# Means stored as whole rows from the edge loops of a graph network, and partitions that load successive rows

## The chip, the cores and the metric

The kernel runs on one core of one Trainium2 chip. The core has five engines that each take their instructions in order and wait for one another by semaphores: TensorE (PE, matrix products and the turning of blocks, with PEld for its weight loads), VectorE (DVE), ScalarE (ACT), GpSimd (POOL, which here issues the gathers from DRAM) and SyncE (SP, which here issues all other DMAs). The metric is the device time of one execution in microseconds. Before the change three runs took 10164.5, 10168.21 and 10176.87 us, the median is 10168.21 us. All values are float32 unless said otherwise.

## What is computed

There are 10,000 nodes with 64 features, and 160,000 directed edges with 64 features each, sorted by target node. A network of four GENConv layers is followed by one attention layer; both have residual connections. What matters here is what happens on the edges:

```python
def _genconv(x, src, dst, ea, W1, b1, lg, lb, W2, b2, t):
    m = relu(x[src] + ea) + EPS
    logits = m * t
    mx = segment_max(logits, dst)
    e = exp(logits - mx[dst])
    denom = segment_sum(e, dst)
    agg = segment_sum(m * (e / denom[dst]), dst)    # a mean of m with weights e
    h = agg + x
    ...

def _L1_gnn_ref(x, edge_attr, edge_index, WQ, bQ, WK, bK, WE, bE, WV, bV):
    ...
    score = Kh[src] * Qh[dst] * inv_sqrt_d * Eh
    score = exp(clip(score.sum(-1, keepdims=True), -5.0, 5.0))
    return segment_sum(Vh[src] * score, dst)
```

Each GENConv layer is an edge part (`softmax_layer`) and a node part (`node_layer`); the attention layer has an edge part (`attention_layer`) and leaves its sums to a last node part.

## The kernel before

**Tiling.** The edges lie in two halves. The first half is read forward on partitions 0 to 63 (one partition for each of the 64 features), the second half is read backward on partitions 64 to 127. So a tile of 128 partitions by 512 columns holds 512 edges of each half. A chunk is such a tile (CE = 512 columns in CG = 4 groups of G = 128). There are NC = 158 chunks: 155 of 512 columns, then two of 256 and one of 128.

**One chunk in `softmax_layer`.** `fetch` issues on SP the loads of `marks` (two DMAs, L797, saying where a new target begins) and of `ea`, the edge features (L766). In layer 0 the features come as rows of edges instead (`load_rows`, L773 and L775); PE turns them into columns (`turn_rows`, L784 and L785), ACT copies them out of PSUM (L788) and SP stores them in `eaT` (L789) for the later layers. `front` issues eight gathers of 128 rows on POOL (`xg`, L756), then PE forms z from the features (L829) and adds the turned gathered rows (L831). ACT makes the logits lg in two operations (L834, L835). A scan on DVE follows the running maximum u (L841), a subtraction (L843) leaves the difference to it, and ACT derives `up` (L846) and e (L848, L849). `decay` makes `dec` on ACT (L856). `back` runs one chunk later on DVE: the weighted message `me` (L869), the scan `se` of the weights (L871) and the scan `sm` of the weighted messages (L874). The last column of a target's run of edges holds its denominator in `se` and its numerator in `sm`. Then two 32 by 32 block transposes (L900) turn both, so that 64 channels of sums and weights of one edge can be stored as a row of `st0` (L904): four DMAs of 32 partitions, each with 512 runs of 256 bytes in a full chunk.

**Buffers.** z has five PSUM banks in layers 1 to 3 (three called z, and `ept` and `hist`), three in layer 0, where the others are in use. `lg`, `dec` and `oe` have one bank each. In SBUF `xg` has 7 buffers, `marks` 6, `ea` 4, `so` 3, `u`, `up`, `e`, `se` and `sm` 2, `me` 1.

**Order.** `InOrder` (L68) holds every engine to the order in which the code emits its instructions. In the loop (L906 to L938) one turn emits: `fetch(k+3)`, `front(k)`, the columns of chunk k+2, in layer 0 the counting of edges for the row indices (one-hot tiles on DVE, products on PE), `back(k-1)`, `decay(k)`.

**`node_layer`.** Gathers, for each group of up to 8 x 128 nodes, the row of `st0` at the node's last edge in each half: sums and weights, 128 numbers (`fetch`, L955). `divide` (L962) takes Ln and Exp of the weights on ACT (L967, L968) and multiplies on DVE (L969). Then follow the layer norms and products. `rows_of_nodes` (L496) works out the row indices (`ends`) once, in layer 0. A node without edges in a half reads the one extra row at the end of `st0`, which holds constants.

**`attention_layer`.** Per chunk: `fetch` loads marks, queries (`q`, L1141, a row for each edge in `qs`) and features; `ahead` turns the queries on PE (L1151), forms the edge part (L1154), scans the queries along the edges (L1156) and multiplies (L1160). `scores` turns the gathered keys and values (`kv`, 8 gathers in two `xg` buffers), multiplies (L1183) and sums over heads on PE (L1185); `weights` clips (L1191) and takes the exponential on ACT (L1192); `back` runs a chunk later: product (L1199), scan (L1201), one transpose (L1212), and four stores (L1216) of 512 runs of 128 bytes into `st1`.

Of the kernel before, what the change touches and what calls it, by code (L numbers as in the profile page):

```python
# [9 lines left out]
F32 = mybir.dt.float32  # L10
# [16 lines left out]
def kernel(ctx: ExitStack, tc: tile.TileContext, a, out):  # L27
# [142 lines left out]
    empty = const.tile([1, D2 + D], F32, name="empty")  # L170
    for h in range(2):
        nc.gpsimd.memset(empty[:, h * D:h * D + 32], 1.0)
        nc.gpsimd.memset(empty[:, h * D + 32:(h + 1) * D], -EPS)
    nc.gpsimd.memset(empty[:, D2:], 0.0)
    zeros = const.tile([P, 500], F32, name="zeros")
    nc.gpsimd.memset(zeros, 0.0)
    later.append((st0[2 * HALF:2 * HALF + 1, :], empty[:, 0:D2]))
    later.append((st1[2 * HALF:2 * HALF + 1, :], empty[:, D2:]))

    def load(name, shape, ap):  # L180
        t = const.tile(shape, F32, name=name)
# [314 lines left out]
    def rows_of_nodes(pool, ph):  # L496

        def t(name):
            return pool.tile([P, NT], F32, name="rn_" + name, bufs=1)
        V = nc.vector  # L500
        cnt = t("cnt")
        V.tensor_copy(cnt, ph)
        upto, before = place_nodes(pool, cnt, "ept")
        some = t("some")
        V.tensor_scalar(some, cnt, 0.0, None, op0=OP.is_gt)
        ra, rb, inb = t("ra"), t("rb"), t("inb")
        V.tensor_scalar(inb, before, float(HALF), None, op0=OP.is_ge)
# [8 lines left out]
        V.tensor_scalar_add(ends, ra, float(2 * HALF))  # L516

        ba, bb, spare = t("ba"), t("bb"), t("spare")
# [250 lines left out]
    def load_rows(k, ea_rows):  # L769
        g0, n, cols = span(k)  # L770
        er = edge.tile([P, 2, CG, D], F32, name="er", bufs=3)
        e1 = NE - g0 * G
        nc.sync.dma_start(er[:, 0, :n, :],  # L773
                          ea_rows[g0 * G:(g0 + n) * G, :].rearrange("(g p) d -> p g d", p=G))
        nc.sync.dma_start(er[:, 1, :n, :],  # L775
                          ea_rows[e1 - n * G:e1, :].rearrange("(g p) d -> p g d", p=G))
        return er

    def turn_rows(k, er):

        g0, n, cols = span(k)
        pt = ps("ept", [P, CE])
        for g in range(n):
            nc.tensor.matmul(pt[:D, g * G:(g + 1) * G], er[:, 0, g, :], ident, start=True, stop=True)  # L784
            nc.tensor.matmul(pt[D:, g * G:(g + 1) * G], er[:, 1, n - 1 - g, :], anti,  # L785
                             start=True, stop=True)
# [11 lines left out]
        return t  # L798

    V, S = nc.vector, nc.scalar  # L800

    def softmax_layer(l, ea_rows=None):

# [61 lines left out]
        def back(k, z, u, dec, e):  # L865
# [11 lines left out]
            if k == NC - 1:  # L877
# [15 lines left out]
                for i, t in ((1, se), (2, sm)):  # L893
                    V.tensor_mul(far[:, i:i + 1], far[:, i:i + 1], top[:, 3:4])
                    V.scalar_tensor_tensor(t[:D, m - 1:m], fin[:D, i:i + 1], top[:, 2:3],
                                           far[:, i:i + 1], op0=OP.mult, op1=OP.add)

            so = edge.tile([P, CE // 32, 2, 32], F32, name="so", bufs=3)
            for i, t in ((0, se), (1, sm)):
                V.transpose(so[:, :m // 32, i, :], t[:, :m].rearrange("p (b e) -> p b e", e=32))  # L900
# [14 lines left out]
        for k in range(NC):  # L915
# [18 lines left out]
            if l == 1 and k % 4 == 0:  # L934
                clear_queries(k // 4)
            order()
        back(NC - 1, *held)
        order()  # L938

    def node_layer(l):  # L940
# [21 lines left out]
        @stage  # L962
        def divide(my, g, i0, n, c):
            q = 2 * pairs(n)
            t = my["g"][:, :q].rearrange("p n (h i c) -> p n h i c", h=2, i=2)
            my["h"] = h = work.tile([P, GRP, D], F32, name="n_h", bufs=2)
            S.activation(t[:, :, :, 0, :], t[:, :, :, 0, :], AF.Ln)  # L967
            S.activation(t[:, :, :, 0, :], t[:, :, :, 0, :], AF.Exp, scale=-1.0)  # L968
            V.tensor_mul(h[:, :q, :].rearrange("p n (h c) -> p n h c", h=2), t[:, :, :, 1, :], t[:, :, :, 0, :])  # L969

        @stage
        def enter(my, g, i0, n, c):
# [128 lines left out]

        for g in range(3):
            fetch(g)
        divide(0)
        for i in range(NG2 + (4 if last else 3)):
            span_narrow(i - 3)
            widen(i - 1)
# [5 lines left out]
            spans(i - 1)  # L1113
            relu_narrow(i - 3)
            square(i - 2)
            divide(i + 1)
            back(i - 3)
            root_wide(i - 1)
            leave(i - 3)
# [14 lines left out]
    def attention_layer():  # L1134
# [3 lines left out]
        def fetch(k):  # L1138
            g0, n, cols = span(k)
            q = edge.tile([P, CG, 2, D], F32, name="q", tag="er", bufs=3)  # L1140
            nc.sync.dma_start(  # L1141
                q[:, :n], qs[2 * g0 * G:2 * (g0 + n) * G, :].rearrange("(g p s) d -> p g s d", p=G, s=2))
            return load_marks(k, keeps_d), q, load_ea(k)

        def ahead(k, keep, q, ea):
# [2 lines left out]
            m = n * G  # L1148
            pq = ps("oe", [P, CE])
            for g in range(n):  # L1150
                nc.tensor.matmul(pq[:, g * G:(g + 1) * G], q[:, g, :, :].rearrange("p s d -> p (s d)"),  # L1151
                                 ident, start=True, stop=True)
# [42 lines left out]
        def back(k, keep, pv, sc):  # L1195
# [8 lines left out]
            if k == NC - 1:  # L1204
# [17 lines left out]
        for k in range(NC):  # L1222
            kvs = fetch_kv(k)
            if k + 2 < NC:
                got.append(fetch(k + 2))
            pv, psc = scores(k, kvs, made)
            if held is not None:
                back(k - 1, *held)
            held = got[k][0], pv, weights(k, psc)
            if k + 1 < NC:  # L1230
                made = ahead(k + 1, *got[k + 1])
            order()
        back(NC - 1, *held)
        order()

    puts = []
# [69 lines left out]
```

## Time and profile before

| what | us |
|---|---|
| median of three runs | 10168.21 |
| the profiled execution: its time | 10256.79 |
| its span on the core | 10254.7 |
| layer 0, first to last scan of u (L841) | 1823.57 |
| layer 1, the same | 1810.51 |
| layer 2, the same | 1804.37 |
| layer 3, the same | 1804.35 |
| attention, first to last scan of its sums (L1201) | 1783.61 |
| mean granted TensorE clock over the span, as a share of full speed | 0.629 |

The five stretches of the table hold 9026 us of the span. Between them lie the node parts, some 190 us each, in which 79 gathers read `st0`. A page of the profile lists busy time by engine, groups of instructions by line and tile, and waits by what ended them; the timeline lists single instructions in the order of their start, with in brackets the idle time of that engine just before. "remote" as the end of a wait means a semaphore of another engine that the records don't tie to one instruction; "issue" means that the profile shows nothing that was waited for.

Single durations that the text uses: ACT operations on 128 by 512 take 0.56 to 0.75 us, on 128 by 256 0.34 to 0.42 us; L843 0.70 us, the transposes of L900 0.67 to 0.69 us, the scans L841, L871 and L874 1.26 to 1.28 us; L967, L968 and L969 0.62, 0.63 and 0.69 us; a gather on POOL 0.94 us.

### The profile page before, as it was taken

The numbers are of one execution on the slowest core, as the hardware profiler recorded it, in microseconds if no ns is written. First come the engines' busy times: TensorE is split into PE (matmuls) and PEld (weight loads), VectorE is DVE, ScalarE is ACT, GpSimd is POOL, SyncE is SP. The second block draws the span as 40 slices with busy tenths as digits, with TensorE's granted clock in tenths as the row PEclk, the third lists the DMA queues.
The fourth block names the chain that finished last, engine by engine and source line by source line (L and its number), as shares of the span: only waits on it lengthen the run. The fifth ranks groups of instructions, "written<-read, shape, count | busy, mean of one in ns | idle before, by whom it ended". The sixth has DMA issues, their size and how long they took to land. (4 is left out here: it accounts for less than half of the span.)

```text
span 10254.7 us, 67417 instructions
## 1 busy us (share of the span) xinstructions
PE 4014.2 (39%) x15762; PEld 2685.3 (26%) x15762; DVE 5449.4 (53%) x7473; ACT 2805.0 (27%) x4803; POOL 6358.1 (62%) x6760
## 2 busy tenths in 40 slices
PE   3554445443333333433333343333333444444452
PEld 2333333222222221222222221222222233333331
DVE  3777677535555554355555543555555445545453
ACT  2333333333333333333333342333333310000000
POOL 4566666556666665566666646666666456666665
PEclk6666666665555556665666575555555667777776
DMA  3555555524555554244444433444444235555553
GB/s 89 113 125 123 123 124 123 123 59 119 125 125 129 128 124 109 62 102 105 104 104 103 105 78 71 105 105 104 103 104 106 62 92 122 125 123 126 122 128 82
DMA packets 2462634, 1103.63 MB, mean 108 GB/s; under 512 B 2039472, under 2 KB 2254438, under 8 KB 2462239
## 3 DMA queue, kind: packets, MB, share of 16 engines
q1 hardware_dynamic: 2247039, 827.14, 33.8%
q0 software_dynamic: 215200, 272.11, 12.6%
q8 instruction: 140, 2.29, 0.1%
q14 instruction: 255, 2.09, 0.1%
HBM read 626.51 MB, written 471.91 MB: 107 GB/s over the span
## 5 line engine op out<-in xcount | busy, mean ns | idle before, releaser
L756 POOL DMA_INDIRECT xg<-table,idxA x2500 | 2358.6, 943 | 1916.9 <-remote 829.7
L756 POOL DMA_INDIRECT xg<-table,idxB x2500 | 2358.8, 944 | 763.1 <-issue 761.2
L841 DVE TENSOR_TENSOR_SCAN u<-lg,u,marks 128x512 f32<-128x512 f32 (+1 forms) x628 | 798.5, 1272 | 2721.5 <-ACT lg L835 1612.7
L829 PE MATMUL z<-ea,eencW 128*128 128x512 f32 (+1 forms) x892 | 864.3, 1071 | 2137.1 <-DMA ea<-eaT 898.3
L831 PEld LDWEIGHTS z<-ident,xg 128*128 128x128 f32 x3512 | 800.4, 311 | 591.8 <-issue 566.5
L756 POOL DMA_INDIRECT kv<-kv_table,idxA x625 | 589.5, 943 | 439.7 <-remote 220.2
L831 PE MATMUL z<-ident,xg 128*128 128x128 f32 x3512 | 794.5, 395 | 162.0 <-DMA xg<-table,idxB 85.9
L829 PEld LDWEIGHTS z<-ea,eencW 128*128 128x128 f32 x892 | 222.2, 306 | 2231.8 <-issue 1981.7
L871 DVE TENSOR_TENSOR_SCAN se<-dec,se,e 128x512 f32<-128x512 f32 (+1 forms) x628 | 792.2, 1261 | 0.0
L874 DVE TENSOR_TENSOR_SCAN sm<-dec,sm,me 128x512 f32<-128x512 f32 (+1 forms) x628 | 782.3, 1246 | 0.0
L846 ACT ACTIVATE up<-lg 128x512 f32<-128x512 f32 (+1 forms) x632 | 374.3, 592 | 1352.9 <-issue 693.6
L756 POOL DMA_INDIRECT kv<-kv_table,idxB x625 | 589.7, 944 | 191.1 <-issue 190.2
L834 ACT ACTIVATE lg<-z 128x512 f32<-128x512 f32 (+1 forms) x446 | 249.4, 559 | 1555.8 <-remote 1032.3
L1185 PE MATMUL dec<-eq,head_sum 128*128 128x512 f32 (+2 forms) x316 | 237.1, 841 | 931.2 <-DVE eq L1183 887.1
L1192 ACT ACTIVATE sc<-sc 128x512 f32<-128x512 f32 (+1 forms) x158 | 98.7, 625 | 1744.7 <-DVE sc L1191 685.0
L784 PE MATMUL ept<-ident,er 128*64 128x128 f32 x1250 | 269.3, 380 | 752.4 <-ACT ea L788 517.7
L856 ACT ACTIVATE dec<-up 128x512 f32<-128x512 f32 (+1 forms) x632 | 377.1, 597 | 658.8 <-issue 561.0
L756 POOL DMA_INDIRECT n_g<-st,ends x316 | 300.8, 952 | 403.2 <-issue 142.2
L835 ACT ACTIVATE lg<-lg,teps,tcol 128x512 f32<-128x512 f32 (+1 forms) x632 | 471.4, 746 | 21.1
L829 PE MATMUL hist<-ea,eencW 128*128 128x512 f32 x186 | 189.5, 1123 | 709.5 <-DMA ea<-eaT 286.6
L829 PE MATMUL ept<-ea,eencW 128*128 128x512 f32 x186 | 185.5, 1100 | 710.3 <-DMA ea<-eaT 286.4
L1156 DVE TENSOR_TENSOR_SCAN qh<-marks,qh,oe 128x512 f32<-128x512 bf16 (+1 forms) x157 | 198.6, 1265 | 488.6 <-remote 389.8
(285 smaller groups left out, 8704.9 us busy)
## 6 DMA issues: line engine op xcount, KB each, us to landing
st<-so SPq DMA_DIRECT2D x2480, 128.0 KB
ea<-eaT SPq DMA_DIRECT2D x620, 256.0 KB
marks<-ends_d SPq DMA_DIRECT2D x1240, 64.0 KB
st<-so SPq DMA_DIRECT2D x652, 64.0 KB
xg<-table,idxA POOLq DMA_INDIRECT x2500
xg<-table,idxB POOLq DMA_INDIRECT x2500
qs<-zeros SPq DMA_DIRECT2D x40, 1000.0 KB
er<-in_edge_attr_dram SPq DMA_DIRECT2D x310, 128.0 KB
```

The source lines that it names most:

```text
L756: nc.gpsimd.indirect_dma_start(out=t, out_offset=None, in_=table, in_offset=bass.IndirectOffsetOnAxis(ap=idx, axis=0))
L784: nc.tensor.matmul(pt[:D, g * G:(g + 1) * G], er[:, 0, g, :], ident, start=True, stop=True)
L829: nc.tensor.matmul(z[:, :m], eencW, ea[:, :m], start=True, stop=False)
L831: nc.tensor.matmul(z[:, g * G:(g + 1) * G], xg[:, g, :, :].rearrange("p s d -> p (s d)"), ident, start=False, stop=(g == n - 1))
L834: S.activation(lg[:, :m], z[:, :m], AF.Relu)
L835: S.activation(lg[:, :m], lg[:, :m], AF.Identity, bias=teps[:, l:l + 1], scale=tcol[:, l:l + 1])
L841: V.tensor_tensor_scan(u[:, 1:m + 1], lg[:, :m], marks[:, :m], last, op0=OP.max, op1=OP.add)
L846: S.activation(up[:, :m], lg[:, :m], AF.Relu)
L856: S.activation(dec[:, :m], up[:, :m], AF.Exp, scale=-1.0)
L871: V.tensor_tensor_scan(se[:, :m], dec[:, :m], e[:, :m], prev.get("e", zero1), op0=OP.mult, op1=OP.add)
L874: V.tensor_tensor_scan(sm[:, :m], dec[:, :m], me[:, :m], prev.get("m", zero1), op0=OP.mult, op1=OP.add)
L1185: nc.tensor.matmul(psc[:, :m], head_sum, eq[:, :m], start=True, stop=True)
```

## The change

1. The edge loop of `softmax_layer` divides already. A new step `mean` takes Ln and Exp(-) of `se` on ACT and multiplies `sm` by it on DVE, for chunk k-2; its space r is the PSUM bank `oe` in layers 1 to 3 and the buffer of `me` in layer 0. One transpose (`turn_sums`) follows instead of two.
2. `st0` holds 64 means per edge, `st1` 64 sums as before, both in a new order: 32 edges of one block column stand on 32 partitions, and a partition's 16 blocks with their 64 channels are 4 KB in a row. For this, ACT copies the other 32 channels beside the first 32 (two copies on 32 partitions, `send_sums`), and two DMAs of 32 rows replace the four. This is emitted one turn later (`send`), for chunk k-3 in the softmax layers and k-2 in attention.
3. In the loop, `send` and `mean` stand before `back(k-1)`; after the loop they are run out.
4. `node_layer` gathers 64 numbers per node straight into `h`; `divide` is gone.
5. `rows_of_nodes` maps the row index to the new order (13 further operations on tiles of 128 by 79). Rows for nodes without edges are the unused blocks of the last chunk's place, set once.
6. `load_rows` and the loads of the queries give one partition four successive edges (1 KB in place of four pieces of 256 bytes; 2 KB for the queries in place of four of 512 bytes); PE's products then write their columns with a stride of four.

```diff
+    NB = -(-HALF // CE)
+    SB = CE // 32
-    st0 = dram.tile([2 * HALF + 1, D2], F32, name="st0")
-    st1 = dram.tile([2 * HALF + 1, D], F32, name="st1")
+    st0 = dram.tile([NB * 64 * SB, D], F32, name="st0")
+    st1 = dram.tile([NB * 64 * SB, D], F32, name="st1")
...
@@ rows_of_nodes
+        V.tensor_single_scalar(part, ends, 10, op=OP.logical_shift_right)
+        V.tensor_scalar(place, part, float(64 * SB), None, op0=OP.mult)
+        for down, keep, times in ((0, 1, 32 * SB), (1, 31, SB), (6, SB - 1, 1)):
...
+            V.scalar_tensor_tensor(place, upper_part, float(times), place, op0=OP.mult, op1=OP.add)
+        V.tensor_copy(ends, place)
@@ load_rows (both halves), and the loads of q alike
-                          ea_rows[g0 * G:(g0 + n) * G, :].rearrange("(g p) d -> p g d", p=G))
+                          ea_rows[g0 * G:(g0 + n) * G, :].rearrange("(p g) d -> p g d", p=G))
@@ turn_rows, and the products of pq alike
+        each = pt[:, :n * G].rearrange("q (p g) -> q g p", g=n)
         for g in range(n):
-            nc.tensor.matmul(pt[:D, g * G:(g + 1) * G], er[:, 0, g, :], ident, start=True, stop=True)
+            nc.tensor.matmul(each[:D, g, :], er[:, 0, g, :], ident, start=True, stop=True)
@@ new
+    def turn_sums(t, m):
+        so = edge.tile([P, SB, 2, 32], F32, name="so", bufs=3)
+        V.transpose(so[:, :m // 32, 0, :], t[:, :m].rearrange("p (b e) -> p b e", e=32))
+        return so
+
+    def send_sums(k, so, st):
+        g0, n = chunks[k]
+        nb, b0 = n * G // 32, g0 * G // 32 % SB
+        rows_of = st.rearrange("(k s e b) d -> k s e b d", s=2, e=32, b=SB)[g0 * G // CE]
+        for s in range(2):
+            p = s * D
+            S.activation(so[p:p + 32, :nb, 1, :], so[p + 32:p + D, :nb, 0, :], AF.Copy)
+            nc.sync.dma_start(rows_of[s, :, b0:b0 + nb, :],
+                              so[p:p + 32, :nb].rearrange("p b h c -> p b (h c)"))
@@ softmax_layer, back
-            so = edge.tile([P, CE // 32, 2, 32], F32, name="so", bufs=3)
-            for i, t in ((0, se), (1, sm)):
-                V.transpose(so[:, :m // 32, i, :], t[:, :m].rearrange("p (b e) -> p b e", e=32))
-            rows_out = st0[2 * g0 * G:2 * (g0 + n) * G, :].rearrange(
-                "(b e s) (h x) -> s h e b x", e=32, s=2, h=2)
-            for q in range(4):
-                nc.sync.dma_start(rows_out[q // 2, q % 2],
-                                  so[q * 32:(q + 1) * 32, :m // 32].rearrange("p b i c -> p b (i c)"))
+            summed.append((k, se, sm))
+
+        def mean():
+            if summed:
+                k, se, sm = summed.pop(0)
+                m = span(k)[1] * G
+                r = ps("oe", [P, CE]) if ph is None else edge.tile([P, CE], F32, name="r", tag="me", bufs=1)
+                S.activation(r[:, :m], se[:, :m], AF.Ln)
+                S.activation(r[:, :m], r[:, :m], AF.Exp, scale=-1.0)
+                mn = edge.tile([P, CE], F32, name="mn")
+                V.tensor_mul(mn[:, :m], sm[:, :m], r[:, :m])
+                turned.append((k, turn_sums(mn, m)))
+
+        def send():
+            if turned:
+                send_sums(*turned.pop(0), st0)
@@ its loop
             if counts and counts[-1][-1] == R * KT:
                 rows_of_nodes(edge, ph)
+            send()
+            mean()
             if held is not None:
                 back(k - 1, *held)
             held = z, u, decay(k, up), e
...
+        send()
+        mean()
         back(NC - 1, *held)
+        send()
+        mean()
+        send()
@@ node_layer, fetch (and the whole of divide, with its calls, is taken out)
-            my["g"] = t = edge.tile([P, GRP, D2], F32, name="n_g", tag="so", bufs=3)
+            my["h"] = t = edge.tile([P, GRP, D], F32, name="n_g", tag="so", bufs=3)
@@ attention_layer, back
-            so = edge.tile([P, CE // 32, 32], F32, name="so1", tag="so", bufs=3)
-            V.transpose(so[:, :m // 32, :], s[:, :m].rearrange("p (b e) -> p b e", e=32))
-            rows_out = st1[2 * g0 * G:2 * (g0 + n) * G, :].rearrange(
-                "(b e s) (h c) -> s h e b c", e=32, s=2, h=2)
-            for q in range(4):
-                nc.sync.dma_start(rows_out[q // 2, q % 2], so[q * 32:(q + 1) * 32, :m // 32])
+            turned.append((k, turn_sums(s, m)))
@@ its loop
             pv, psc = scores(k, kvs, made)
+            send()
             if held is not None:
                 back(k - 1, *held)
```

More of the change, by code (lines that the diff above doesn't have):

```diff
@@ L169 @@
     nc.vector.memset(neg1, NEG)
[L170 to L174, printed above, removed]
+    empty = const.tile([64, 2 * D], F32, name="empty")
+    nc.gpsimd.memset(empty[:, :D], -EPS)
+    nc.gpsimd.memset(empty[:, D:], 0.0)
     zeros = const.tile([P, 500], F32, name="zeros")
     nc.gpsimd.memset(zeros, 0.0)
-    later.append((st0[2 * HALF:2 * HALF + 1, :], empty[:, 0:D2]))
-    later.append((st1[2 * HALF:2 * HALF + 1, :], empty[:, D2:]))
+    assert HALF % CE
+    used = HALF // 32 % SB
+    for i, st in enumerate((st0, st1)):
+        later.append((st.rearrange("(k p b) d -> k p b d", p=64, b=SB)[NB - 1, :, used:, :],
+                      empty[:, None, i * D:(i + 1) * D].to_broadcast([64, SB - used, D])))
     def load(name, shape, ap):
@@ L516, in rows_of_nodes @@
         V.tensor_scalar_add(ends, ra, float(2 * HALF))
+        part, upper_part = pool.tile([P, NT], I32, name="rn_part", bufs=1), t("upper")
+        place = t("place")
+        V.tensor_single_scalar(part, ends, 10, op=OP.logical_shift_right)
+        V.tensor_scalar(place, part, float(64 * SB), None, op0=OP.mult)
+        for down, keep, times in ((0, 1, 32 * SB), (1, 31, SB), (6, SB - 1, 1)):
+            of = ends
+            if down:
+                V.tensor_single_scalar(part, ends, down, op=OP.logical_shift_right)
+                of = part
+            V.tensor_single_scalar(part, of, keep, op=OP.bitwise_and)
+            V.tensor_copy(upper_part, part)
+            V.scalar_tensor_tensor(place, upper_part, float(times), place, op0=OP.mult, op1=OP.add)
+        V.tensor_copy(ends, place)
         ba, bb, spare = t("ba"), t("bb"), t("spare")
@@ L773, in load_rows @@
         nc.sync.dma_start(er[:, 0, :n, :],
-                          ea_rows[g0 * G:(g0 + n) * G, :].rearrange("(g p) d -> p g d", p=G))
+                          ea_rows[g0 * G:(g0 + n) * G, :].rearrange("(p g) d -> p g d", p=G))
         nc.sync.dma_start(er[:, 1, :n, :],
-                          ea_rows[e1 - n * G:e1, :].rearrange("(g p) d -> p g d", p=G))
+                          ea_rows[e1 - n * G:e1, :].rearrange("(p g) d -> p g d", p=G))
         return er
@@ L782, in turn_rows @@
         pt = ps("ept", [P, CE])
+        each = pt[:, :n * G].rearrange("q (p g) -> q g p", g=n)
         for g in range(n):
-            nc.tensor.matmul(pt[:D, g * G:(g + 1) * G], er[:, 0, g, :], ident, start=True, stop=True)
-            nc.tensor.matmul(pt[D:, g * G:(g + 1) * G], er[:, 1, n - 1 - g, :], anti,
-                             start=True, stop=True)
+            nc.tensor.matmul(each[:D, g, :], er[:, 0, g, :], ident, start=True, stop=True)
+            nc.tensor.matmul(each[D:, g, :], er[:, 1, n - 1 - g, :], anti, start=True, stop=True)
         ea = edge.tile([P, CE], F32, name="ea", bufs=4)
@@ L800 @@
     V, S = nc.vector, nc.scalar
+    def turn_sums(t, m):
[5 more added lines that the diff above has]
+        nb, b0 = n * G // 32, g0 * G // 32 % SB
+        assert b0 + nb <= SB
+        rows_of = st.rearrange("(k s e b) d -> k s e b d", s=2, e=32, b=SB)[g0 * G // CE]
[4 more added lines that the diff above has]
+                              so[p:p + 32, :nb].rearrange("p b h c -> p b (h c)"))
     def softmax_layer(l, ea_rows=None):
@@ L896, in back @@
                                            far[:, i:i + 1], op0=OP.mult, op1=OP.add)
-            so = edge.tile([P, CE // 32, 2, 32], F32, name="so", bufs=3)
-            for i, t in ((0, se), (1, sm)):
-                V.transpose(so[:, :m // 32, i, :], t[:, :m].rearrange("p (b e) -> p b e", e=32))
-            rows_out = st0[2 * g0 * G:2 * (g0 + n) * G, :].rearrange(
-                "(b e s) (h x) -> s h e b x", e=32, s=2, h=2)
-            for q in range(4):
-                nc.sync.dma_start(rows_out[q // 2, q % 2],
-                                  so[q * 32:(q + 1) * 32, :m // 32].rearrange("p b i c -> p b (i c)"))
+            summed.append((k, se, sm))
[12 more added lines that the diff above has]
+                send_sums(*turned.pop(0), st0)
+        summed, turned = [], []
         order = InOrder()
@@ L960, in fetch @@
                 V.memset(t[:, n, :], 1.0)
[L962 to L969, printed above, removed]
         @stage
@@ L1103, in node_layer @@
             fetch(g)
-        divide(0)
         for i in range(NG2 + (4 if last else 3)):
@@ L1115, in node_layer @@
             square(i - 2)
-            divide(i + 1)
             back(i - 3)
@@ L1141, in fetch @@
             nc.sync.dma_start(
-                q[:, :n], qs[2 * g0 * G:2 * (g0 + n) * G, :].rearrange("(g p s) d -> p g s d", p=G, s=2))
+                q[:, :n], qs[2 * g0 * G:2 * (g0 + n) * G, :].rearrange("(p g s) d -> p g s d", p=G, s=2))
             return load_marks(k, keeps_d), q, load_ea(k)
@@ L1150, in ahead @@
             for g in range(n):
-                nc.tensor.matmul(pq[:, g * G:(g + 1) * G], q[:, g, :, :].rearrange("p s d -> p (s d)"),
-                                 ident, start=True, stop=True)
+                nc.tensor.matmul(pq[:, :m].rearrange("q (p g) -> q g p", g=n)[:, g, :],
+                                 q[:, g, :, :].rearrange("p s d -> p (s d)"), ident, start=True, stop=True)
             pe = ps("hist", [P, CE])
@@ L1210, in back, with send @@
                                        op0=OP.mult, op1=OP.add)
-            so = edge.tile([P, CE // 32, 32], F32, name="so1", tag="so", bufs=3)
-            V.transpose(so[:, :m // 32, :], s[:, :m].rearrange("p (b e) -> p b e", e=32))
-            rows_out = st1[2 * g0 * G:2 * (g0 + n) * G, :].rearrange(
-                "(b e s) (h c) -> s h e b c", e=32, s=2, h=2)
-            for q in range(4):
-                nc.sync.dma_start(rows_out[q // 2, q % 2], so[q * 32:(q + 1) * 32, :m // 32])
+            turned.append((k, turn_sums(s, m)))
+        turned = []
+        def send():
+            if turned:
+                send_sums(*turned.pop(0), st1)
         order = InOrder()
@@ L1232, in attention_layer @@
             order()
+        send()
         back(NC - 1, *held)
+        send()
         order()
```

## The prediction

> **What bounds the kernel now.** First the busy totals with the five edge stages as windows (each from its first to its last DVE scan: layers 1, 0 and the attention layer are shown; layers 2 and 3 take 1804.37 and 1804.35); columns are the window, its length, then PE, PEld, DVE, ACT, POOL busy, the granted clock, the DMA engines' share and GB/s.
>
> ```profile
> PE 4014.2 (39%) x15762; PEld 2685.3 (26%) x15762; DVE 5449.4 (53%) x7473; ACT 2805.0 (27%) x4803; POOL 6358.1 (62%) x6760
> 2186.43:3996.94 1810.51, 574.66 (x1555) 372.83 (x1554) 960.94 (x1251) 560.06 (x942) 1168.89 (x1240) 0.57 0.51 122
> 177.80:2001.37 1823.57, 894.59 (x5296) 640.05 (x5296) 1285.16 (x1877) 643.00 (x1108) 1125.45 (x1193) 0.65 0.56 122
> 8354.34:10137.95 1783.61, 878.90 (x4328) 651.14 (x4326) 918.91 (x1097) 98.11 (x157) 1144.21 (x1213) 0.74 0.53 124
> ```
>
> The five stages hold 9026 of the 10254.7 us. No engine fills one of them and DMA is half used: the time is in waits. POOL comes nearest: in the timeline its gathers start every 1.249 us, eight to a chunk, so 9.98 us a chunk and 1561 us a layer of 1250. Second, the waits:
>
> ```profile
> ACT lg L834 <- remote: 1794.8, 145, 22.5
> POOL xg L756 <- remote: 829.7, 134, 13.0
> ```
>
> ACT stands at the first operation of a chunk for a semaphore of PE. Third, the timeline at the end of one such wait:
>
> ```profile
> 4595.19 1.91 PE L831 MATMUL ept<-ident,xg 128*128 128x128 f32 x8
> ...
> 4602.25 0.58 ACT L834 ACTIVATE lg<-z 128x512 f32<-128x512 f32 x1 [15.62 <-remote]
> 4602.48 0.94 POOL L756 DMA_INDIRECT xg<-table,idxA  x1 [8.65 <-remote]
> ```
>
> PE has had its matmuls out for 5 us; ACT and POOL are let go together, after POOL has stood still for 8.65 us. This repeats: the start-to-start times of the scan L841 in layers 1 to 3 run in a cycle of six chunks, four of 6.9 us, one of 18.0, one of 22.6, together 68.2 us. That is 48 gathers (59.95 us) and one stop of POOL (8.4). So PE's news seems to get through late while POOL streams, and the pace, 11.4 us a chunk, is POOL's own plus its stops. At the start of layers 1 to 3 POOL has seven buffers to fill and no stop, and the first seven intervals take 145 us.
>
> Fourth, a chunk that waits for nothing, in the timeline:
>
> ```profile
> 3010.15 0.60 ACT L856 ACTIVATE dec<-up 128x512 f32<-128x512 f32 x1 [1.21 <-issue]
> 3010.68 0.55 ACT L834 ACTIVATE lg<-z 128x512 f32<-128x512 f32 x1
> 3011.27 0.75 ACT L835 ACTIVATE lg<-lg,teps,tcol 128x512 f32<-128x512 f32 x1
> 3012.05 1.28 DVE L841 TENSOR_TENSOR_SCAN u<-lg,u,marks 128x512 f32<-128x512 f32 x1 [0.71 <-ACT lg L835]
> 3013.38 0.70 DVE L843 TENSOR_TENSOR lg<-lg,u 128x512 f32<-128x512 f32 x1
> 3013.98 0.68 DVE L869 SCALAR_TENSOR_TENSOR me<-z,e 128x512 f32<-128x512 f32 x1
> 3014.11 0.60 ACT L846 ACTIVATE up<-lg 128x512 f32<-128x512 f32 x1 [2.08 <-issue]
> 3014.58 1.27 DVE L871 TENSOR_TENSOR_SCAN se<-dec,se,e 128x512 f32<-128x512 f32 x1
> 3014.60 0.59 ACT L848 ACTIVATE e<-lg 128x512 f32<-128x512 f32 x1
> 3015.22 0.63 ACT L849 ACTIVATE e<-e 128x512 f32<-128x512 f32 x1
> 3015.77 1.26 DVE L874 TENSOR_TENSOR_SCAN sm<-dec,sm,me 128x512 f32<-128x512 f32 x1
> 3016.95 0.69 DVE L900 STREAM_TRANSPOSE so<-se 128x512 f32<-128x512 f32 x1
> 3017.06 0.60 ACT L856 ACTIVATE dec<-up 128x512 f32<-128x512 f32 x1 [1.21 <-DVE sm L874]
> ```
>
> dec has one bank, so dec(k) waits until sm(k-1) has read dec(k-1); ACT takes lg(k+1) only behind dec(k); DVE takes me(k-1) only behind the subtraction of k. This ring of ACT and DVE takes 6.91 us, with both transposes hidden under ACT's part. It is not the bound today; the other 4.5 us of a mean chunk are waits for PE.
>
> **The change, part by part: the edge loops.** DVE's order becomes u(k), subtraction(k), mean product and one transpose of k-2, me, se, sm of k-1. ACT's order becomes lg, lg, up, e, Exp of e, two copies, Ln, Exp, dec. The product waits for ACT's last Exp, and behind it on DVE are me, se and sm, for which dec waits, and behind dec the next chunk. So the ring now goes through all of it. Start-to-start steps from the rows above: dec to lg 0.53, lg 0.59, u 0.78, subtraction 1.33, up 0.73, e 0.49, Exp 0.62, together 5.07 to the start of that Exp. New: to the first copy 0.53, second copy 0.53, Ln 0.53 (the step of independent ACT operations, as dec to lg), its Exp 0.62 (as e to Exp), to the product 0.63 (that Exp's duration): 2.84. Then product to transpose 0.72 (0.70 of L843), transpose to me 0.60, se 0.60, sm 1.19, dec 1.29: 4.40. Sum 12.31 us. The copies touch 32 partitions and no row shows such a copy. Were they as short as ACT's 64x2 operations in the trace (0.2 us), the ring would be 11.65; were each of the new steps a whole duration, 12.5. I take 0.53, for their 512 columns are those of the rows.
>
> The Trainium skill, ScalarE: Activation LUTs, "What ACT_TABLE_LOAD costs", has an operation pay for columns (one element per cycle and lane) and nothing for partitions. The rows agree as to columns (0.60 us at 512, 0.38 at 256); none here varies partitions. By the page the ring stays 12.31, by the shortest row 11.65.
>
> In layers 1 to 3, POOL at 9.98 and SP with two stores fewer stay under 12.31; POOL must now stop some 14 us in six chunks, more than the 8.4 that let PE's news through, and five z banks cover 60 us of ring, so I add no wait. The first seven chunks are POOL streaming, where the ring isn't the limit: I keep 145 us (the other bound is seven rings, 86). One layer: 145, 146 x 12.31 = 1797, and 36 for the last four intervals (short chunks, 22.8 today) make 1978; three are 5934 against 5419: **+515**.
>
> In layer 0 the ring also holds the copy of ea on ACT and the one-hots on DVE. From rows around 1013 us: u to subtraction 1.33, 0.73, 0.49, 0.62, ea copy 0.53, then 0.55, 0.53, 0.53, 0.62, 0.66 to the product, 0.72, 0.60, 0.60, 1.19 to sm, and 3.39 from sm through the one-hots to u: 13.09 us, 12.9 once the counting ends. 139 x 13.09 + 14 x 12.9 + 38 = 2039 against 1824: **+215**.
>
> The stores: 2 issues of 32 rows of 4 KB in place of 4 issues of 512 runs of 256 B. On SP they wait for ACT's copies; behind them are loads for three chunks on, with 37 us in hand.
>
> ```profile
> DMA packets 2462634, 1103.63 MB, mean 108 GB/s; under 512 B 2039472, under 2 KB 2254438, under 8 KB 2462239
> ```
>
> Nearly all of those small packets are these stores. What their going gives is a gain only where the ring isn't the limit: the starts (0 to -177) and the attention layer.
>
> The Trainium skill, DMA: Bandwidth & Descriptors, "Specifications", asks for 512 B or more and has less read, modified and written. By it the stores are what the layers wait for, and the sum would be POOL's 9.98 a chunk; the row speaks against, with DMA engines 44 to 56% busy and 28% at the starts, where the waits are longest.
>
> **Attention.** Its loop gains two copies on ACT (98 us busy of 1784) and loses two issues; the transposes no longer hold the same turn's stores. Bounds: 0, and 1561 - 1784 = -222 if nothing but POOL were left. I take 0: its waits have the form above (a gather at 9026.49 after 3.60 us of "remote"), at starts and stores alike.
>
> **The rest.** Node layers lose two ACT and one DVE operation per group (0.62, 0.63, 0.69), about 2 us at their start, and wait about as much longer for the last two chunks' means: 0 (-20 to +10 in all). Rows read four at a time as 1 KB: loads three chunks ahead, hidden. PE writing with a stride: 0, as PE is 49% busy in layer 0; at four times the 270 us of L784 it would have 810 more, 1704 of 1824, and still fit. Thirteen small DVE operations for row numbers: +3. The one ACT table load of the trace stays one.
>
> Sum: 515 + 215 + 3 = 733. The profiled run took 10256.79 us, 0.9% over the median of the runs; the differences are put on the median, 10168: **10,900**.
>
> **Rivals.** A second slower case: the small packets are what delays PE's news, so starts and attention come free too: 733 - 177 - 222, or 10,500. For it: SP's issues go at 0.7 us in the slow stretches and 0.5 in quick ones; against: SP is silent in whole stretches of waiting. A third, slower still: PE's news stays late and part of the wait comes on top of the ring. The mean chunk has 4.46 us over its fast form; a quarter to a third kept is 1.1 to 1.5 us on 440 chunks and 0.8 to 1.1 on 150, 600 to 820 more: about 11,600. On the other side, faster: the stores' packets set the pace everywhere and the added 5.4 us of ring fit inside what the waits (4.46) leave, or the ring is looser than I read it. Each edge stage then falls to POOL's 1561 to 1567: 718 + 257 + 222 less, about 9,000. It decides from a ring under 11.4 us; it needs the five new ACT steps in under 1.9 us instead of 2.84, against the rows. That the rows of 4 KB are cut up again on the way, so that the stores change nothing, leaves the forecast as it is.
>
> **How the numbers follow.** Forecast 0.66, own range 10,500 to 11,010 (a ring of 11.65 takes 0.66 x 590 chunks = 390 off, one of 12.5 adds 110). Freed starts and attention 0.16, waits on top 0.10, faster 0.06, no difference 0.02. Under 0.2% is what a measurement of this kernel can't tell from none. The range 10,450 to 11,300 takes in the second case and leaves the outer ones: 0.8. Slower 0.92, same 0.02, faster 0.06.
>
> **What would show it.** Scan L841 to scan in layers 1 to 3 every 12.3 us with little scatter, 13.1 in layer 0; the product's wait on DVE ended by ACT's Exp; ACT's "remote" waits at lg nearly gone after the seventh chunk; POOL waiting 2.3 us a chunk; packets under 512 B down by more than half; attention unchanged. Wrong it would be if the scans came faster than 11.4 us, if attention lost 100 us, or if remote waits stayed beside the ring.

## The result, and the profile after

The change makes the kernel slower: 11251.83 us (median of four runs, 11238.98 to 11256.69) against 10167.32 us of the kernel before beside it, a ratio of 1.1063 with a 95% interval of 1.1044 to 1.1082. The prediction was 10,900 us, in a range of 10,450 to 11,300.

From the page of the changed kernel: the span, the busy time by engine, the DMA packets, and the group of the new copies (which lie at L837; the other lines have moved too).

```profile
span 11237.2 us, 69225 instructions
PE 4017.2 (36%) x15762; PEld 2689.1 (24%) x15762; DVE 5535.8 (49%) x7439; ACT 4475.5 (40%) x7551; POOL 6361.4 (57%) x6757
DMA packets 710166, 929.87 MB, mean 83 GB/s; under 512 B 256013, under 2 KB 431874, under 8 KB 709755
L837 ACT ACTIVATE so<-so 32x512 f32<-32x512 f32 (+1 forms) x1580 | 982.9, 622 | 43.1 <-DVE so L826 2.8
```

Packets under 512 bytes fell from 2.04 million to 0.26 million, and ACT has 1670 us more to do. Yet no engine fills the span: POOL comes nearest with 57%. The same stretches as before, layer 1, layer 0 and attention (columns as in the prediction):

```profile
2505.93:4547.10 2041.17, 582.91 (x1555) 377.98 (x1554) 990.42 (x1249) 931.53 (x1560) 1168.90 (x1239) 0.57 0.34 90
178.69:2324.54 2145.85, 875.95 (x5296) 632.63 (x5296) 1306.57 (x1889) 1025.04 (x1726) 1127.76 (x1193) 0.64 0.31 84
9337.97:11120.49 1782.52, 882.87 (x4328) 653.68 (x4326) 918.13 (x1096) 293.69 (x470) 1143.80 (x1213) 0.75 0.45 124
```

Layer 1 is 231 us longer (layers 2 and 3 237 each, both 2041.1), layer 0 322 us longer; attention is the same within some 1 us. DVE is busy 30 us more in layer 1 and ACT 371 us more, at the same POOL work. The waits that show where the time is:

```profile
POOL xg L776 <- PE z L870: 1233.5, 342, 23.7
DVE mn L947 <- ACT oe L944: 1020.1, 235, 4.4
ACT lg L873 <- remote: 93.1, 6, 22.5
```

ACT's "remote" wait at the first operation of a chunk has gone from 1794.8 to 93.1 us (all its waits there, whatever they are put down to, from 2489 to 302). In its place DVE stands at the new product for ACT, 4.4 us in a full chunk of layers 1 to 3; the profile spreads these waits over five lines, the longest of which is shown, together 2807 us in 631 waits. POOL, the pacemaker of before, waits for PE. One chunk of layer 1 in the timeline, nearly all of the ring:

```profile
3009.26 0.63 ACT L888 ACTIVATE e<-e 128x512 f32<-128x512 f32 x1
3009.91 1.28 ACT L837 ACTIVATE so<-so 32x512 f32<-32x512 f32 x2
3011.22 0.60 ACT L944 ACTIVATE oe<-se 128x512 f32<-128x512 f32 x1
3011.85 0.58 ACT L945 ACTIVATE oe<-oe 128x512 f32<-128x512 f32 x1
3012.46 0.69 DVE L947 TENSOR_TENSOR mn<-sm,oe 128x512 f32<-128x512 f32 x1 [4.35 <-ACT oe L944]
3013.18 0.71 DVE L826 STREAM_TRANSPOSE so<-mn 128x512 f32<-128x512 f32 x1
3013.82 0.65 DVE L908 SCALAR_TENSOR_TENSOR me<-hist,e 128x512 f32<-128x512 f32 x1
3014.40 1.26 DVE L910 TENSOR_TENSOR_SCAN se<-dec,se,e 128x512 f32<-128x512 f32 x1
3015.58 1.25 DVE L913 TENSOR_TENSOR_SCAN sm<-dec,sm,me 128x512 f32<-128x512 f32 x1
3016.87 0.60 ACT L895 ACTIVATE dec<-up 128x512 f32<-128x512 f32 x1 [4.44 <-issue]
3017.40 0.55 ACT L873 ACTIVATE lg<-z 128x512 f32<-128x512 f32 x1
3017.99 0.75 ACT L874 ACTIVATE lg<-lg,teps,tcol 128x512 f32<-128x512 f32 x1
...
3020.15 0.94 POOL L776 DMA_INDIRECT xg<-table,idxA  x1 [2.48 <-PE hist L870]
```

The two engines take turns. DVE idles 4.35 us before the product while ACT does e, Exp, two copies, Ln and Exp; then ACT idles 4.44 us before dec while DVE does the product, the transpose, me, se and sm. The scans of u stand 12.68 us apart, in layers 1 to 3 with hardly any scatter after the start (10th to 90th percentile 12.68 to 12.69). POOL stands still 2.48 us in the chunk shown.

### The profile page after: what moved, and what is told of

Its sections match the earlier page's. It is cut to its first block, busy times and chain, and to the rows that moved or that the text cites. A ratio compares the mean times of both kernels' runs of the same rounds, so it can differ in the third digit from the quotient of the medians.

```text
span 11237.2 us, 69225 instructions
## 1 busy us (share of the span) xinstructions
PE 4017.2 (36%) x15762; PEld 2689.1 (24%) x15762; DVE 5535.8 (49%) x7439; ACT 4475.5 (40%) x7551; POOL 6361.4 (57%) x6757
## 4 chain that ended last, share of the span: by engine, by line
DVE 27%; ACT 24%; issue 21%; PE 10%; another core or an unknown queue 9%; DMA 3%; POOL 2%; SPq 2%; ACTq 0%; DVEq 0%; POOLq 0%
ACT so L837 7%; DVE u L880 6%; DVE sm L913 5%; DVE so L826 3%; DVE lg L882 3%; ACT up L885 3%; ACT lg L874 3%; ACT dec L895 2%; DVE me L908 2%; ACT e L887 2%; ACT oe L944 2%; ACT lg L873 2%; PE z L868 2%; DMA ea<-eaT 2%
## 5 line engine op out<-in xcount | busy, mean ns | idle before, releaser
L868 PE MATMUL z<-ea,eencW 128*128 128x512 f32 (+1 forms) x892 | 898.5, 1111 | 2597.1 <-DMA ea<-eaT 2116.6
L947 DVE TENSOR_TENSOR mn<-sm,oe 128x512 f32<-128x512 f32 (+1 forms) x474 | 323.0, 682 | 2033.2 <-ACT oe L944 1020.1
L837 ACT ACTIVATE so<-so 32x512 f32<-32x512 f32 (+1 forms) x1580 | 982.9, 622 | 43.1 <-DVE so L826 2.8
L870 PEld LDWEIGHTS z<-ident,xg 128*128 128x128 f32 x3512 | 836.5, 324 | 589.2 <-issue 560.0
L870 PE MATMUL z<-ident,xg 128*128 128x128 f32 x3512 | 826.8, 410 | 123.0 <-DMA xg<-table,idxB 84.9
L947 DVE TENSOR_TENSOR mn<-sm,r 128x512 f32<-128x512 f32 (+1 forms) x158 | 108.5, 686 | 773.5 <-issue 417.8
```

Of the source, the lines that this page charges most:

```text
L837: S.activation(so[p:p + 32, :nb, 1, :], so[p + 32:p + D, :nb, 0, :], AF.Copy)
L868: nc.tensor.matmul(z[:, :m], eencW, ea[:, :m], start=True, stop=False)
L870: nc.tensor.matmul(z[:, g * G:(g + 1) * G], xg[:, g, :, :].rearrange("p s d -> p (s d)"), ident, start=False, stop=(g == n - 1))
L947: V.tensor_mul(mn[:, :m], sm[:, :m], r[:, :m])
```

## The experiments

Each run has its own runs of the kernel before beside it. These took 10,186 us at the median in the first set, 10,258 in the second and 10,181 in the third, so ratios, not times, are compared between sets. "Start" below is the sum of the first seven intervals between scans of u (L841 before) in a layer, "steady" the mean interval from there to the last four; both are read from the starts in the timeline.

**The same work in another order (e1_order).** In the loop:

```diff
             send()
-            mean()
+            divide()              # Ln and Exp on ACT
             if held is not None:
                 back(k - 1, *held)
+            mean()                # product and transpose on DVE
             held = z, u, decay(k, up), e
```

In layer 0, r also gets a buffer of its own here, in place of that of `me`.

> The change with its mean split in the order of work: Ln and Exp stay on ACT ahead of dec, the product and the transpose go behind sm on DVE (r gets a buffer of its own in layer 0). Same operations, same stores. Theory (the ring of ACT and DVE sets the pace because the product stands between the subtraction and me): the way from the subtraction to dec becomes ACT's own, 0.73+0.49+0.62+0.65+0.66+0.66+0.63+0.60 = 5.04 us, with 3.23 from dec to the subtraction the ring is 8.3 us, under the 11.1 us at which the kernel before ran after its start. So layers 1 to 3 return to some 1805 us each, layer 0 to some 1825 to 1850 (ring 10.5), the time to 10,100 to 10,200 us. Rival 1 (it is the added amount of ACT and DVE work, not its place): stays at 11,200. Rival 2 (small packets held the kernel before back, and their going helps once the ring is open): layers fall toward 1570 to 1650 us, the time to 9,500 or less.

Measured: 10242.98 us, ratio 1.0059 (1.0043 to 1.0076). In the timeline of layer 2:

```profile
4407.08 1.28 ACT L837 ACTIVATE so<-so 32x512 f32<-32x512 f32 x2
4408.38 0.60 ACT L944 ACTIVATE oe<-se 128x512 f32<-128x512 f32 x1
4409.02 0.58 ACT L945 ACTIVATE oe<-oe 128x512 f32<-128x512 f32 x1
4409.51 0.60 ACT L895 ACTIVATE dec<-up 128x512 f32<-128x512 f32 x1
4409.63 0.69 DVE L953 TENSOR_TENSOR mn<-sm,oe 128x512 f32<-128x512 f32 x1 [1.40 <-ACT oe L944]
```

dec now follows ACT's last Exp at once, and the product runs beside it. The ring is 8.16 us where it shows (the shortest and most frequent interval), 8.3 had been expected; the steady mean is 11.22 to 11.23 us in layers 1 to 3, as in the kernel before (11.20 to 11.25). Nearly the whole loss was the order: the added work alone costs 0.6%. The other half of the finding is that nothing is won either: a ring of 6.9 and one of 8.2 us give the same pace in layers 1 to 3.

**The copies out of the ring (e2_fourstores).**

```diff
-        for s in range(2):
-            p = s * D
-            S.activation(so[p:p + 32, :nb, 1, :], so[p + 32:p + D, :nb, 0, :], AF.Copy)
-            nc.sync.dma_start(rows_of[s, :, b0:b0 + nb, :], ...)
+        for q in range(4):
+            h = q % 2 * 32
+            nc.sync.dma_start(rows_of[q // 2, :, b0:b0 + nb, h:h + 32], so[q * 32:(q + 1) * 32, :nb, 0, :])
```

> The change without its two copies on ACT: four DMAs of 512 runs of 128 B store the means from their own partitions, in both loops. Theory: two copies of 0.655 us leave the ring, 12.68 becomes 11.37 us in layers 1 to 3 and 13.46 becomes 12.15 in layer 0, in spite of the small packets: about 10,480 us. Rival (the number of small packets counts): the ring is shorter but the time doesn't follow, 11,000 us or more, with ACT's waits for PE back in steady running.

Measured: 10470.27 us, ratio 1.0279 (1.0258 to 1.0299); the most frequent interval 11.25 us in layers 1 to 3 and 12.0 in layer 0, against 12.68 and 13.46. The theory's 10,480 holds, with four small stores back. The mean is 11.43 to 11.47 us in layers 1 to 3, some 0.2 over the ring and over the 11.2 of before: where the two are nearly equal, a little comes on top. The two copies cost 1.43 us of ring, more than their 1.28 us of busy time, for without them Ln follows Exp sooner:

```profile
4415.98 0.63 ACT L886 ACTIVATE e<-e 128x512 f32<-128x512 f32 x1
4416.51 0.58 ACT L942 ACTIVATE oe<-se 128x512 f32<-128x512 f32 x1
```

The step is 0.53 us here; from Exp to a copy, from copy to copy and from a copy to Ln it is 0.65 us (3009.26 to 3011.22 above). The copies overlap with neither neighbour.

**Whole rows without anything else (e3_wholerows).** In the kernel before, for `st0` and in the same way for `st1`:

```diff
-            rows_out = st0[2 * g0 * G:2 * (g0 + n) * G, :].rearrange(
-                "(b e s) (h x) -> s h e b x", e=32, s=2, h=2)
+            rows_out = st0[2 * g0 * G:2 * (g0 + n) * G, :].rearrange("(q p x) d -> q p (x d)", q=4, p=32)
             for q in range(4):
-                nc.sync.dma_start(rows_out[q // 2, q % 2], ...)
+                nc.sync.dma_start(rows_out[q], ...)
```

> The kernel before, with each of its four stores written as 32 rows of 4 KB (2 KB in the attention layer) in place of 512 runs of 256 or 128 B, to the same rows of the chunk but in another order, so that the nodes read other edges' sums. Same bytes, same number of DMAs, same dependences. Theory (PE's news comes through late while POOL streams; packets have no part): L841 to L841 stays at a mean of 11.1 us after a start of 145 us, 10,100 to 10,200 us. Rival (small packets set the pace): the stages fall toward POOL's 1561 us, 9,000 to 9,600 us, starts from 145 toward 90 us.

Measured: 10200.86 us, ratio 1.0015 (1.0006 to 1.0025). Its packets, its layer 2 as a window, and ACT's wait:

```profile
DMA packets 963754, 1103.63 MB, mean 108 GB/s; under 512 B 439472, under 2 KB 655334, under 8 KB 963359
4164.00:5958.08 1794.08, 577.96 (x1555) 375.52 (x1554) 960.91 (x1252) 559.84 (x942) 1169.02 (x1239) 0.57 0.43 102
ACT lg L834 <- remote: 1917.2, 163, 22.5
```

1.6 million small packets fewer, and yet the layer (1804 before) and its start (145.3 us) hardly move, and ACT's waits don't shrink. The small packets, which the change removes, did not limit the kernel before; both rivals of the prediction that rested on them fall, and with them the account by which the layers wait for these stores.

**The chain without the copies (e4_chain).** The kernel before with this put ahead of `back(k-1)`, its result unused:

```diff
+                S.activation(r[:, :m], se[:, :m], AF.Ln)
+                S.activation(r[:, :m], r[:, :m], AF.Exp, scale=-1.0)
+                mn = edge.tile([P, CE], F32, name="mn")
+                V.tensor_mul(mn[:, :m], sm[:, :m], r[:, :m])
```

> The kernel before with Ln, Exp and the product put where the change has them, their result left unused; no copies, the old transposes and stores. Theory (ring and POOL's pace work side by side, the longer one counts): ring 12.68 less copies 1.31 less the transpose ahead of me 0.72 = 10.65 us, under 11.1, so layers 1 to 3 stay near 1805 to 1830 us; in layer 0 the two transposes now stand behind the product and before the one-hots, 13.46 - 1.31 - 0.72 + 1.37 = 12.8 us, +180 us: about 10,350 us. Rival (waits come on top of the ring): 3.7 us more in each chunk, about 12,300 us.

Measured: 10487.58 us, ratio 1.0296 (1.0275 to 1.0316). The ring of layers 1 to 3 is 10.53 us (10.65 expected), and their steady mean is 11.30 to 11.33: an addition of 3.6 us to the ring of 6.9 moved the mean by 0.1. Layer 0's ring is 12.6 us, over its floor, and there the mean went from 11.76 to 12.69. So the ring and the floor work side by side and the longer one counts; the third case of the prediction, waits on top of the ring, falls. The spans of the profiled executions differ by 230 us, 158 of it in layer 0 and 25 to 30 in each of layers 1 to 3, the medians by 301; 180 had been expected.

**What the floor is.** The floor of some 11.2 us was the same with rings of 6.9, 8.2 and 10.5 us. Three runs change e1_order's buffers and loads. f1_xg4 and f2_xg9 change the number of buffers of `xg`, which the node parts' `kvq` and the attention layer's `kv` share:

```diff
-            xg = edge.tile([P, CG, 2, D], F32, name="xg", bufs=7)
+            xg = edge.tile([P, CG, 2, D], F32, name="xg", bufs=4)     # f2_xg9: 9
```

> The reordered change (e1_order) with 4 gather buffers in place of 7, so that POOL can be 4 chunks ahead of PE. Theory (the floor of 11.2 us a chunk is POOL's own: it streams six chunks, 59.9 us, then stops some 8 us until PE's news is through): it now stops after three chunks, (29.96 + 8.2) / 3 = 12.7 us a chunk in layers 1 to 3, some 650 us more in all, and the first seven intervals of a layer, in which POOL streamed without a stop, fall under 145 us. Rival (the floor comes from the loads on SP or from a fixed cost outside POOL): 11.2 us a chunk as before, 10,240 us.

> The reordered change with 9 gather buffers. Theory of POOL's stops: eight chunks between stops, (79.9 + 8.2) / 8 = 11.0 us a chunk, about 90 us less than e1_order's 10,243; but the start, where POOL streams, gets longer (two more chunks at some 28 us a layer), so 10,150 to 10,400. Rival (nothing of POOL's): no change.

f1_xg4: 10221.43 us, ratio 0.9966 (0.9953 to 0.9979). f2_xg9: 10409.44 us, ratio 1.0150 (1.0133 to 1.0167). Half of each expectation held. The starts go with the buffers: 102 to 112 us with 4, 145 with 7, 163 to 165 with 9. But the floor hardly moves, 11.42 to 11.47 with 4 and 11.32 to 11.35 with 9, and with 4 buffers too POOL stops every six chunks, for 9.1 us on average (8.5 with 7). So my account of the stops, that POOL runs out of buffers after six chunks, is wrong.

f3_lead4 issues loads earlier:

```diff
-        lead = 3
+        lead = 4
```

> The reordered change with the loads of marks, features and rows issued four chunks ahead in place of three, and one more buffer each for features and rows (marks have six already). Theory of POOL's stops: no change, 10,240 us. Rival (PE waits for the features' load, 900 us of its waits in the kernel before): the floor of 11.2 us falls toward POOL's 9.98, up to 700 us less.

Measured: 10310.47 us, ratio 1.0057 (1.0040 to 1.0074), as e1_order's. Issuing the loads earlier wins nothing. It does change the rhythm: most stops of POOL now come after seven chunks and are longer (below).

Two runs took work away from e1_order, six gathers a chunk for eight (h1_gathers6), and two of PE's four products with gathered rows (h2_products2):

```diff
-            for g in range(n):
+            for g in range(min(n, 3)):                  # h1_gathers6; PE reads xg[:, g % 3]
                 for s in range(2):
                     gather(xg[:, g, s, :], tables[l], index(g0 + g, s))
...
             for g in range(n):
+                if g % 2 or n == 1:                     # h2_products2
```

> The reordered change (e1_order) with six gathers in place of eight in a chunk of the softmax layers; PE's products of the fourth group read the first group's rows again, so the fourth group's messages are those of other edges. Theory (POOL's gathers make the floor of 11.2 us): 7.5 us of gathers and the stop's 1.4 a chunk, 8.9 us in layers 1 to 3, the ring's 10.5 in layer 0: some 1,150 us less, about 9,050 us. Rival (PE, or the loads on SP, make the floor): 10,240 us.

> The reordered change with all eight gathers, but PE adds only every second group's turned rows (two products with weight loads in place of four a chunk), so half the edges' messages lack the node's part. Theory (POOL): no change, 10,200 to 10,260 us. Rival (PE is slower than its records show, and its work makes the floor): 11.2 us falls toward POOL's 9.98 or the ring's 8.2, 9,300 to 9,700 us.

h1_gathers6: 8777.92 us, ratio 0.8619 (0.8602 to 0.8636). h2_products2: 10230.97 us, ratio 1.0046 (1.0030 to 1.0062). Layer 2 as a window, e1_order first, then h1_gathers6, then h2_products2:

```profile
4190.18:6002.79 1812.61, 584.04 (x1555) 379.14 (x1554) 991.51 (x1249) 919.70 (x1560) 1168.92 (x1239) 0.57 0.33 79
```

```profile
3560.38:4953.69 1393.31, 562.47 (x1555) 368.85 (x1554) 991.48 (x1250) 917.88 (x1560) 880.40 (x931) 0.59 0.39 95
```

```profile
4175.94:5982.04 1806.10, 453.19 (x935) 247.62 (x934) 991.45 (x1249) 918.60 (x1560) 1168.92 (x1239) 0.54 0.34 79
```

With a quarter of the gathers gone the steady mean falls from 11.23 to 8.6 us, close to the ring's 8.16, with all of PE's, DVE's and ACT's work in place. With PE's products halved it doesn't fall (11.55 to 11.61); the starts do, from 145 to 90 us, and the two cancel in the time. The floor is POOL's gathers, though h1_gathers6 doesn't tell their issue on POOL from their transfers. 1,150 us less had been expected for h1_gathers6; against its own comparison it is 1,403, or 1,465 from e1_order's median.

The stops go with the gathers as well. Three of them, in f1_xg4 after 48 gathers, in f3_lead4 after 56 and in h1_gathers6 after 24:

```profile
4730.55 0.94 POOL L776 DMA_INDIRECT xg<-table,idxA  x1 [9.25 <-PE hist L870]
```

```profile
5017.06 0.94 POOL L776 DMA_INDIRECT xg<-table,idxA  x1 [10.83 <-PE z L870]
```

```profile
4201.43 0.95 POOL L776 DMA_INDIRECT xg<-table,idxA  x1 [4.79 <-remote]
```

The mean stop in layers 1 to 3 is 4.6 us after 24 gathers (h1_gathers6), 8.5 after 48 (e1_order) and 10.4 after 56 (f3_lead4). From one stop to the next that makes 1.42 to 1.43 us a gather in all three, where gathers without a stop start every 1.25 us. So how often POOL stops doesn't set the pace: the time lost grows with the number of gathers. What it is spent on no run shows.

**The strided loads alone (g1_loads).** The kernel before with this, and the queries alike:

```diff
-                          ea_rows[g0 * G:(g0 + n) * G, :].rearrange("(g p) d -> p g d", p=G))
+                          ea_rows[g0 * G:(g0 + n) * G, :].rearrange("(p g) d -> p g d", p=G))
...
-            nc.tensor.matmul(pt[:D, g * G:(g + 1) * G], er[:, 0, g, :], ident, start=True, stop=True)
+            nc.tensor.matmul(each[:D, g, :], er[:, 0, g, :], ident, start=True, stop=True)
```

> The kernel before with the sixth part of the change alone: a partition reads four successive edges' rows or queries, and PE writes its columns with a stride. Prediction's step: costs and gains nothing, 10,150 to 10,210 us, with the products of the turned rows as long as before (380 ns). Rival: PE's strided writes are slower, layer 0 and attention grow; or layer 0's loads were late, and layer 0 falls under 1,800 us.

Measured: 10257.76 us, ratio 1.0001 (0.9991 to 1.0010). The products of the turned rows take 384 ns with the stride, 380 without. This part does nothing to the time.

**Fewer gather buffers without the means (h3_before_xg4, h4_xg5).** The kernel before with 4 gather buffers, and e1_order with 5:

> The kernel before with 4 gather buffers in place of 7. If the gain of f1_xg4 over e1_order is the shorter start (145 to 105 us in each of three layers), the same comes here, 60 to 120 us less than the kernel before, and the floor stays 11.2 us; if it needs the means in the loop, nothing changes here.

> The reordered change with 5 gather buffers. Between f1_xg4 (ratio to the kernel before 0.9966) and e1_order (1.0059): starts of some 120 us, floor unchanged; layer 0 and the attention layer, which lost 28 and 24 us with 4 buffers, keep more of their pace. 0.993 to 1.001.

h3_before_xg4: 10089.02 us, ratio 0.9904 (0.9888 to 0.9921). h4_xg5: 10171.16 us, ratio 0.9987 (0.9978 to 0.9997), with starts of 116 to 119 us. Both are within what had been expected. In h3_before_xg4 the starts take 102.4 to 102.8 us for 145 and the layers 1770 to 1775, at a steady mean of 11.25 to 11.28. It is the fastest version found that does the whole work, and beats the kernel before by 1%; the means in the loop are not part of it.

## Why the prediction held, point by point

- **The bound of before.** POOL's gathers with their stops: shown by h1_gathers6 (fewer gathers, faster) and h2_products2 (fewer products, not faster). That PE's news gets through late while POOL streams was read from the times of the waits; the starts that go with the number of buffers fit it. But with half of PE's products the start falls too, to 90 us, so PE has a part in it. That POOL stops because its buffers are full fails by f1_xg4 and f2_xg9; that a stop grows with the gathers ahead of it is shown, and the reason is open.
- **The ring.** The mechanism was right: product and transpose ahead of me, ACT's chain ahead of dec (e1_order undoes the order and 10.0 of the 10.6% go). Its size was 12.31 us by the prediction and 12.68 by the trace. The step that failed is "to the first copy 0.53, second copy 0.53, Ln 0.53": these three took 1.96 us for 1.59, the whole 0.37 that is missing. I had used the step of ACT operations that overlap. The upper bound of 12.5, each new step a whole duration of some 0.60, was too low as well: a copy takes 0.627, and its step of 0.65 is longer still. In layer 0 the same 0.37 makes 13.46 of 13.09.
- **The sum.** 0.37 us on 4 x 146 chunks is 216 us. The last four intervals of a layer took 44.6 to 45.6 us and not 36 to 38: 33. Layer 0 has another 45 in its start, in the turns that also encode the nodes (14.2 us each, and one of 33.4 after them) and in the one at which the counting ends (22.9); the sum had put them all at the ring's length. The node parts were put at 0, between -20 and +10, and gave back 43: the stretches between the stages and ahead of layer 0 sum to 1068.7 us for 1111.5. The median moved by 1084.5 us where the spans of the two profiled executions differ by 982.5, since the one of before was 0.9% over the median of its runs: 102 more. Together that is some 350 us, what the prediction fell short.
- **The range.** The case that came true had its own range, 10,500 to 11,010, and the 11,252 measured lies above it. Only the wider range, whose upper end of 11,300 was set to leave out the third case and was not added up, holds the result: the mechanism was foreseen, that the number fell inside is in part luck.
- **The starts.** Kept at 145 us; measured 145 in each of the three layers.
- **Attention.** Kept the same; measured 1782.52 for 1783.61. In e3_wholerows, with the stores alone, it is 1764.7, 1% less; the 222 us that the second case hoped for don't come.
- **The packets.** Nearly all of the 2.04 million small ones were taken for the stores'; by e3_wholerows 1.6 million are. It bears on nothing, since their going won nothing.
- **Strided writes and loads** at 0: right, by g1_loads. The lost divide and the row numbers: in the 43 us of the node parts, not told apart.
- **The rivals.** The second case (starts and attention freed) and the fast case fall with e3_wholerows; the third (waits on top of the ring) with e4_chain.

## What to carry to other kernels

Before adding work to a loop of two engines that take turns, follow the ring through its single-buffered tiles: the same operations cost 10.6% in one place and 0.6% in another, where the waiting engine had time. As long as the ring is shorter than what another engine needs for the chunk, its length costs next to nothing (here 0.1 us a chunk from 6.9 to 10.5 us), and shortening it wins nothing either. And a large number of small packets is not yet a limit: try the stores alone, scrambled if need be, before moving arithmetic to make them larger.

## What was not expected of the hardware

A copy of 32 partitions by 512 columns from SBUF to SBUF takes 0.627 us on ACT, no less than most operations on 128 partitions (0.55 to 0.63), and starts 0.65 us from its neighbours on both sides, where other independent pairs on ACT are 0.49 to 0.54 us apart. Why these copies don't overlap was not tried. And 4 gather buffers instead of 7 made the kernel before faster by 1% (92 us), for the starts of three layers shrank by some 43 us each.

POOL's stops were the third surprise: each gather cost 1.42 to 1.43 us from stop to stop, whether POOL stopped after 24, 48 or 56 of them.
